# Gate and up projections as 2x2x2 Strassen block products, with weight sums kept in memory

## The chip, the cores and the metric

The kernel runs on one NeuronCore of a Trainium2 chip. The metric is the device time of the program in microseconds (us), as the median of several runs. The core has a matrix engine (TensorE, PE in the profile, with its weight loads as PEld), a vector engine (VectorE, DVE), a scalar engine (ScalarE, ACT), a general engine (GpSimd, POOL) and a sync engine (SyncE, SP), which here issues nearly all DMA transfers. Each engine runs its own instructions in a fixed order and waits on semaphores for the others.

## The reference

The input is x with 2048 rows (2 x 1024) of 1024 values; all data are fp32.

```python
s = silu(x @ w_gate.T)                      # 2048 x 2752
s[the 1376 smallest |s| of each row] = 0    # top-k by rows, k = 0.5 * 2752
s = s * (x @ w_up.T)
x = layernorm(x + s @ w_down.T)
# second part, with weights of a quarter of the width tiled four times,
# and low-rank terms of rank 2
g = silu(qlora(x, w1q, a1, b1)) * qlora(x, w3q, a3, b3)
x = layernorm(x + qlora(g, w2q, a2, b2))
```

The first part has the three large matrix products (2048 x 1024 x 2752 twice, and 2048 x 2752 x 1024); the second part needs a quarter of such work, because the tiled weights let the input be folded first.

## The kernel before, in words

Rows are worked in 16 tiles of 128, in four groups of four tiles (`GT`). The time line has three stages: gate and up for all groups, then the down projection with the first layer norm, then the second part (called FFN below).

**Precision.** TensorE multiplies in the reduced format fp32r. Each fp32 operand is therefore split in two: `split` (L162, L163) casts to fp32r on ScalarE (`xh`, `wh`) and subtracts the cast from the original for the residue (`xl`, `wl`), on GpSimd unless another engine is named. Each product is then three matmuls: high by high, low by high, high by low.

**Gate and up.** The 2752 columns are eight blocks of 344 (`BW`), the 1024 inputs are eight chunks of 128. For each group, each block and each of the two matrices, `gu_w` loads the weight block (three transfers of 3, 3 and 2 chunks), and splits it. `gate_up` then does 24 matmuls (L214) for each of the four tiles. Two tiles share a PSUM pair; there are three pairs. ScalarE takes gate's pair out of PSUM with Silu (L218), VectorE takes up's pair and multiplies it with the Silu result (L223), and both are stored in scratch memory (`s_d`, `m_d`). Weights are split anew for each group. A weight block is prepared while the one before it is multiplied.

**Top-k.** When a group's Silu results are stored, `topk` reads them back for four tiles. It looks for each row's threshold in six passes: three tiles are counted by ScalarE (L259), the fourth by VectorE (L256), and some ten instructions on 128x4 or 128x8 elements (L262 to L282) compute the next guess, for which the next pass waits. Then VectorE picks the exact threshold (L286, L287) and writes the mask (L298), stored as bf16. Top-k of a group runs beside gate and up of the next; the last group's runs beside the down projection.

**Down.** `down_load` (L447) multiplies a product tile by its mask on GpSimd, `down_prep` transposes it (L463) and splits it (L467, L468), and `down_mm` multiplies it with the split down weights (L483) and adds to an accumulator (L486). A small queue (`item`) runs loads two items and preparation some three items ahead.

**Order of the work.** The order in which each engine meets its instructions comes from the framework's scheduler, which works from the program order, the buffers of each pool and its own model of durations. It is fixed before the kernel runs.

Of the kernel before, what the change touches and what calls it, by code (L numbers as in the profile page):

```python
# [26 lines left out]
RW = 3 * BW  # L27
XS = 6
AHEAD = 5
DB = (512, 512, 512, 384, 384, 448)  # L30
GT = 4
EPS = 1e-5
# [4 lines left out]
TKAT = (5, 5, 5)  # L37
WARM = 14
TAILC = ((0, 512), (512, 768), (768, 1024))


class Kern:
# [6 lines left out]
    def run(self):  # L49
# [3 lines left out]
        with ExitStack() as es:  # L53
# [3 lines left out]
            self.sm = es.enter_context(tc.tile_pool(name="sm", bufs=4))  # L57
# [8 lines left out]
            self.k_d = [self.dram.tile([P, NI], BF, name=f"k_d{t}") for t in range(nt)]  # L66
            self.iota = self.const.tile([P, 8], F, name="iota")
            for i in range(8):
                nc.gpsimd.memset(self.iota[:, i : i + 1], 2.0 * i + 2.5)
            self.x_d = [self.dram.tile([P, H], F, name=f"x_d{t}") for t in range(nt)]  # L70
            tk_es, dp_es = ExitStack(), ExitStack()
            self.tk = tk_es.enter_context(tc.tile_pool(name="tk", bufs=1, side="right"))
            self.wp = es.enter_context(tc.tile_pool(name="wp", bufs=1))
            self.ev = es.enter_context(tc.tile_pool(name="ev", bufs=2))
            self.q1, self.q2, self.x2 = [], [], {}
            pst = es.enter_context(tc.tile_pool(name="pst", bufs=2, space=PSUM))
            self.tpb = lambda: pst.tile([P, 4, P], F, tag="tp", name="tp")
            gx_es = [ExitStack(), ExitStack()]
            psm = es.enter_context(tc.tile_pool(name="psm", bufs=3, space=PSUM))
            self.pair = lambda: psm.tile([P, 2, 512], F, tag="mm", name="mm")  # L80
            gx = [
                e.enter_context(tc.tile_pool(name=n, bufs=1, side=sd))
                for e, n, sd in zip(gx_es, ("gx1", "gx2"), ("right", "left"))
            ]
            self.xt = lambda sl, n: gx[sl // 4].tile([P, KC, P], R, tag=f"{n}{sl}", name=n)
            self.xr = gx[1]
# [3 lines left out]
            groups = self.groups(0)  # L90
            slots = self.x_slots(groups)
            d0 = self.down(0, early=3)
            hooks = {(g + 1, b): (lambda g=g: self.topk(g)) for g, b in enumerate(TKAT)}
            hooks[ng - 1, NB - 2] = lambda: next(d0)
            self.items = [(g, b, w) for g in range(ng) for b in range(NB) for w in "gu"]
            xs = self.x_load(groups[0], slots[0])
            for g in range(ng):
                if g == ng - 1:
                    gx_es[1].close()
                    self.dp = dp_es.enter_context(tc.tile_pool(name="dp", bufs=1, reuse_waits="tile"))  # L100
                nx = []
                for b in range(NB):
                    if b == NB - 2 and g + 1 < ng:
                        nx = self.x_load(groups[g + 1], slots[g + 1])
                    self.gate_up(g, b, groups[g], xs)
                    if (g, b) in hooks:
                        hooks[g, b]()
                xs = nx
            gx_es[0].close()
            self.dp2 = dp_es.enter_context(tc.tile_pool(name="dp2", bufs=1, reuse_waits="tile"))  # L110
            list(d0)
            for g in range(1, ng - 1):
                list(self.down(g, hooks={1: lambda: self.topk(ng - 1)} if g == 1 else {}))
            tk_es.close()
# [7 lines left out]

    def groups(self, g0):
        return [range(t, t + GT) for t in range(g0 * GT, self.nt, GT)]

    @staticmethod
    def x_slots(phases):
        free, last, res = list(range(XS)), [], []
        for g in phases:
            order = free + last  # L130
            use = order[: len(g)]
            free = [q for q in order if q not in use and q not in last]
# [32 lines left out]
    def x_load(self, tiles, slots):  # L165
        nc = self.nc
        xs = []
        for t, sl in zip(tiles, slots):
            if t == 2:
                self.nxt = self.gu_w(*self.items[0])  # L170
# [613 lines left out]
```

## Time and profile before

| What | Value |
|---|---|
| Runs before | 2018.61 to 2022.16 us, median 2019.07 (3 runs) |
| Profiled execution | 2021.57 us, of which the span from first to last instruction is 2019.8 |
| Gate and up, first to last matmul of L214 | 7.4 to 979 us |
| Down and first layer norm | to about 1555 us |
| TensorE busy | 1947.3 us, 96% of the span |
| VectorE, ScalarE, GpSimd busy | 1064.9, 897.5 and 1033.9 us |
| DMA | 389.64 MB, 193 GB/s on average |

All times in the profile are of one execution. Busy time of TensorE counts overlapping matmuls once; the length of one matmul in it is a latency, so the rate is to be read from counts in a stretch. A group line gives the source line, the engine, the operation, output and inputs, shape and count, then total busy time and the mean in ns of one, then the idle time just before these instructions and what ended it.

### The profile page before, as it was taken

How to read it: one execution, taken by the hardware profiler on the slowest of the kernel's cores; microseconds unless marked ns; L12 is line 12 of the kernel's file. 1: busy time of each engine (PE TensorE's matmuls, PEld its weight loads, DVE VectorE, ACT ScalarE, POOL GpSimd, SP SyncE). 2: the span in 40 equal slices, each digit the busy share in tenths (PEclk: the TensorE clock that was granted, in tenths of full speed). 3: DMA queues.
4: the chain of work that ended last, by engine and by line, in shares of the span. 5: the costliest groups of instructions: out<-in, count | busy, mean ns of one | idle time of the engine just before them, and what ended most of it. 6: DMA issues, size and time to landing. Idle time of an engine off the chain costs nothing. (4 is left out here: it accounts for less than half of the span.)

```text
span 2019.8 us, 29520 instructions
## 1 busy us (share of the span) xinstructions
PE 1947.3 (96%) x11117; PEld 1807.9 (90%) x11117; DVE 1064.9 (53%) x1581; ACT 897.5 (44%) x1472; POOL 1033.9 (51%) x694
## 2 busy tenths in 40 slices
PE   9999999999999999999988998999999899899998
PEld 9999999999999999999866786788877889899896
DVE  3000056602574024811479845644598987979565
ACT  4222396224952258322663113323323766747363
POOL 3343445454353444543556767555685744626162
PEclk9999999999999999999999998999999999999999
DMA  6555454575546555375644578655556748576561
GB/s 226 177 168 179 155 172 150 189 240 173 173 148 225 189 193 169 119 262 196 224 135 122 173 273 287 230 170 183 172 169 251 252 156 304 185 272 180 200 212 63
DMA packets 165886, 389.64 MB, mean 193 GB/s; under 512 B 16773, under 2 KB 76293, under 8 KB 165737
## 3 DMA queue, kind: packets, MB, share of 16 engines
q1 hardware_dynamic: 165592, 387.45, 57.9%
q8 instruction: 87, 1.43, 0.3%
q14 instruction: 63, 0.51, 0.1%
q10 hardware_dynamic: 144, 0.26, 0.0%
HBM read 297.94 MB, written 89.65 MB: 192 GB/s over the span
## 5 line engine op out<-in xcount | busy, mean ns | idle before, releaser
L163 POOL TENSOR_TENSOR wl<-wr,wh 128x1032 fp32r<-128x1032 f32 (+2 forms) x281 | 662.4, 2382 | 550.9 <-ACT wh L162 550.4
L214 PE MATMUL mm<-wh,xh 128*128 128x344 f32 x2048 | 650.1, 319 | 2.3 <-ACT xh L162 1.8
L214 PE MATMUL mm<-wl,xh 128*128 128x344 f32 x2048 | 651.3, 320 | 0.2 <-POOL wl L163 0.2
L214 PE MATMUL mm<-wh,xl 128*128 128x344 f32 x2048 | 650.7, 319 | 0.4 <-DVE xl L163 0.4
L162 ACT CAST wh<-wr 128x1032 fp32r<-128x1032 f32 (+2 forms) x289 | 274.5, 970 | 481.8 <-PE mm L214 270.3
L214 PEld LDWEIGHTS mm<-wh,xh 128*128 128x128 f32 x2048 | 385.1, 188 | 3.1 <-ACT xh L162 2.1
L214 PEld LDWEIGHTS mm<-wl,xh 128*128 128x128 f32 x2048 | 384.7, 188 | 0.5 <-POOL wl L163 0.4
L214 PEld LDWEIGHTS mm<-wh,xl 128*128 128x128 f32 x2048 | 384.0, 188 | 0.6 <-DVE xl L163 0.6
L223 DVE TENSOR_TENSOR sv<-mm,ev 128x688 f32<-128x688 f32 x64 | 55.5, 871 | 456.1 <-PE mm L214 360.6
L483 PE MATMUL mm<-wh,mh 128*128 128x512 f32 x704 | 231.7, 410 | 11.8 <-DVE acc L486 8.1
L483 PE MATMUL mm<-wl,mh 128*128 128x512 f32 x704 | 225.5, 401 | 10.2 <-POOL wl L163 10.2
L483 PE MATMUL mm<-wh,ml 128*128 128x512 f32 x672 | 213.5, 399 | 0.0
L259 ACT ACTIVATE k<-a,cur 128x2752 bf16<-128x2752 f32 x72 | 186.3, 2588 | 40.9 <-DVE cur L282 24.4
L447 POOL TENSOR_TENSOR m<-m,u 128x512 f32<-128x512 f32 (+2 forms) x96 | 110.6, 1158 | 149.8 <-DMA m<-m_d 94.7
L685 POOL TENSOR_TENSOR hf<-hf,gt 128x344 f32<-128x344 f32 x96 | 141.2, 1480 | 83.1 <-DVE gt L679 78.8
L672 PE MATMUL mm<-wh,fh 128*128 128x344 f32 x512 | 168.7, 330 | 14.3 <-DVE gt L679 8.8
L483 PEld LDWEIGHTS mm<-wl,mh 128*128 128x128 f32 x704 | 132.9, 191 | 43.3 <-POOL wl L163 13.0
L486 DVE TENSOR_TENSOR acc<-acc,mm 128x1024 f32<-128x1024 f32 x96 | 116.4, 1213 | 95.3 <-PE mm L483 94.5
L674 PE MATMUL mm<-wh,fl 128*128 128x344 f32 x512 | 165.7, 324 | 0.0
L673 PE MATMUL mm<-wl,fh 128*128 128x344 f32 x512 | 165.4, 323 | 0.0
L483 PEld LDWEIGHTS mm<-wh,mh 128*128 128x128 f32 x704 | 128.9, 192 | 38.6 <-issue 8.4
L483 PEld LDWEIGHTS mm<-wh,ml 128*128 128x128 f32 x672 | 128.0, 191 | 29.6
(153 smaller groups left out, 2494.4 us busy)
## 6 DMA issues: line engine op xcount, KB each, us to landing
wr<-wd SPq DMA_DIRECT2D x84, 512.0 KB
wr<-wg SPq DMA_DIRECT2D x64, 516.0 KB
wr<-wu SPq DMA_DIRECT2D x64, 516.0 KB
s_d<-ev SPq DMA_DIRECT2D x64, 344.0 KB
m_d<-sv SPq DMA_DIRECT2D x64, 344.0 KB
a<-s_d SPq DMA_DIRECT2D x64, 344.0 KB
wl<-wc_w SPq DMA_DIRECT2D x48, 344.0 KB
wh<-wc_w SPq DMA_DIRECT2D x48, 344.0 KB
```

The source lines that it names most:

```text
L162: self.nc.scalar.copy(hi, raw)
L163: (eng or self.nc.gpsimd).tensor_tensor(lo, raw, hi.bitcast(F), ALU.subtract)
L214: nc.tensor.matmul(o, l, r, start=n == 0, stop=n == len(ops) - 1)
L223: nc.vector.tensor_tensor(m, ps[:, :, :BW], sv[pr], ALU.mult)
L259: nc.scalar.activation(kv[2], av[j], AF.Sign, bias=t, scale=-1.0, accum_out=s)
L447: nc.gpsimd.tensor_tensor(m[:, :w], m[:, :w], u[:, :w], ALU.mult)
L483: nc.tensor.matmul(ps[:, h], a, b[:, h * 512 : (h + 1) * 512], start=i == 0, stop=i == len(ops) - 1)
L486: nc.vector.tensor_tensor(out, out, ps.rearrange("p a b -> p (a b)"), ALU.add)
L672: nc.tensor.matmul(o, fh[:, c, :], wh[:, c, :], start=c == 0, stop=False)
L673: nc.tensor.matmul(o, fh[:, c, :], wl[:, c, :], start=False, stop=False)
L674: nc.tensor.matmul(o, fl[:, c, :], wh[:, c, :], start=False, stop=False)
L685: G.tensor_tensor(hf[:, hs], hf[:, hs], gt, ALU.add)
```

## The change

The product of a 2 x 2 block matrix with another takes eight block products, or seven by Strassen's scheme (here in Winograd's form, with sums that build on each other). The change applies this to gate and up. The input's blocks are the two tiles of a pair (rows) by the two halves of the 1024 inputs; the weight's blocks are the two halves of the inputs by two neighbouring blocks of 344 columns. A *unit* is one matrix (`g` or `u`), two column blocks (`u`, four of them) and one group; it has seven *steps*, each one product for both tile pairs: 2 x 4 chunks x 3 = 24 matmuls into one PSUM pair.

- **Weights.** Each step has one operand of 128 x 1376 (four chunks of 344): three are quarters of the weight, four are sums T1 to T4 (`T_AT`), and all are split by `split` in `w_prep`, cast on ScalarE and residue on GpSimd, three steps ahead (`AHEAD`). In group 0 VectorE makes the sums from the four loaded quarters, and they are stored in scratch memory (`tw_d`); the other groups load them (`w_load`, six steps ahead, five raw buffers).
- **Input.** `x_slot` makes the sums S1 to S4 on VectorE for each pair and splits seven operands of 128 x 512, with the residue on VectorE.
- **Output.** `post` adds the products to four quarters of the result in SBUF: a copy on ScalarE at the first step and seven additions on VectorE after the others, each with one input from PSUM. `finish` applies Silu, or multiplies up's result with gate's, on 128 x 1376 in SBUF, and stores.
- **Buffers.** All of PSUM is used as four pairs in this stage. To make room, the top-k mask is kept as bytes instead of bf16; in the down stage ScalarE turns each mask tile into bf16 before GpSimd multiplies with it. Weight buffers come from rings (`Ring`); the sums and raw inputs borrow top-k's tiles. A few pools are smaller (`sm` three deep for four, the down stage's product tiles four for five).

The core of the diff; line by line it also replaces pools and tags.

```diff
-XS = 6
-AHEAD = 5
+NU = NB // 2
+KH = KC // 2
+CW = KH * BW
+AHEAD = 3
+LOADS = 6
...
+STEPS = (
+    ("A11", "B11"), ("S2", "T2"), ("S3", "T3"), ("S1", "T1"), ("A12", "B21"), ("S4", "B22"), ("A22", "T4"),
+)
+T_AT = ([("T1", "B12", "B11")], [("T2", "B22", "T1")], [("T3", "B22", "B12"), ("T4", "B21", "T2")], [], [], [], [])
...
+    def x_slot(self, g, op):
...
+            a11, a12, a21, a22, t = self.xraw[p]
+            if op == "S2":
+                V.tensor_tensor(t, a21, a22, ALU.add)
+                V.tensor_tensor(a21, a11, a21, ALU.subtract)
+                V.tensor_tensor(a11, t, a11, ALU.subtract)
+            elif op == "S4":
+                V.tensor_tensor(t, a12, a11, ALU.subtract)
+            src = {"A11": a11, "S2": a11, "S1": t, "A12": a12, "S3": a21, "S4": t, "A22": a22}[op]
+            hl = [self.xp.tile([P, KH, P], R, tag=f"{n}{op}{p}", name="x" + n) for n in "hl"]
+            self.split(*(x.rearrange("p a b -> p (a b)") for x in hl), src, V)
...
+    def w_load(self, i):
...
+        if g == 0:
+            if k == 0:
+                self.wb = {q: load(q) for q in ("B11", "B12", "B22", "B21")}
+            self.wraw.append(self.wb)
+        elif b[0] == "T":
+            r = self.wr.get()
+            nc.sync.dma_start(r, self.tw_d[w, u][:, int(b[1]) - 1])
+            self.wraw.append(r)
+        else:
+            self.wraw.append(load(b))
...
+    def w_prep(self, i):
...
+            for o, x, y in T_AT[k]:
+                V.tensor_tensor(tt[o], raw[x], raw.get(y, tt.get(y)), ALU.subtract)
+            if k == 2:
+                for j in range(2):
+                    nc.sync.dma_start(self.tw_d[w, u][:, 2 * j : 2 * j + 2], self.tt[j])
...
+        self.split(hi, lo, raw, V if b in LOV else nc.gpsimd)
...
+            for p in range(NPR):
+                xh, xl = self.xs[p, a]
+                ops[0] += [(p, x[:, q], wh[:, q]) for q in range(KH) for x in (xh, xl)]
+                ops[1] += [(p, xh[:, q], wl[:, q]) for q in range(KH)]
...
+        if k == 0:
+            nc.scalar.copy(c11, x)
+        elif k == 1:
+            V.tensor_tensor(c12, x, c11, ALU.add)
+        elif k == 2:
+            V.tensor_tensor(c21, x, c12, ALU.add)
+        elif k == 3:
+            V.tensor_tensor(c12, x, c12, ALU.add)
+            V.tensor_tensor(c22, x, c21, ALU.add)
+        elif k == 4:
+            V.tensor_tensor(c11, x, c11, ALU.add)
+        elif k == 5:
+            V.tensor_tensor(c12, x, c12, ALU.add)
+            self.finish(un, cc, 0)
+        else:
+            V.tensor_tensor(c21, x, c21, ALU.add)
+            self.finish(un, cc, 1)
...
+        if w == "g":
+            self.nc.scalar.activation(c, c, AF.Silu)
+        else:
+            s = cc[g, u, "g"][t].rearrange("p a b n -> p a (b n)")
+            self.nc.vector.tensor_tensor(c, c, s, ALU.mult)
...
         nc.sync.dma_start(m[:, :w], self.m_d[t][:, i0 : i0 + w])
         nc.sync.dma_start(u[:, :w], self.k_d[t][:, i0 : i0 + w])
-        nc.gpsimd.tensor_tensor(m[:, :w], m[:, :w], u[:, :w], ALU.mult)
+        nc.scalar.copy(ub[:, :w], u[:, :w])
+        nc.gpsimd.tensor_tensor(m[:, :w], m[:, :w], ub[:, :w], ALU.mult)
```

## The prediction

> **What bounds the kernel now.** I read the totals first, then busy time by stretch, the groups by shape for the engines that the change loads, the waits, and last single instructions of two engines side by side.
>
> ```profile
> PE 1947.3 (96%) x11117; PEld 1807.9 (90%) x11117; DVE 1064.9 (53%) x1581; ACT 897.5 (44%) x1472; POOL 1033.9 (51%) x694
> 100.00:200.00 100.00, 100.00 (x638) 100.00 (x637) 6.12 (x7) 23.05 (x28) 45.19 (x21) 1.00 0.54 173
> 300.00:400.00 100.00, 99.76 (x635) 99.47 (x634) 63.12 (x79) 44.35 (x44) 51.00 (x21) 1.00 0.48 156
> 1000.00:1100.00 100.00, 85.22 (x375) 66.53 (x374) 81.19 (x99) 53.72 (x55) 63.85 (x45) 0.95 0.46 139
> 1100.00:1200.00 100.00, 94.75 (x430) 76.17 (x429) 72.06 (x91) 21.79 (x31) 65.83 (x46) 0.97 0.62 211
> 1200.00:1300.00 100.00, 92.43 (x412) 73.80 (x411) 64.84 (x86) 30.58 (x42) 71.82 (x57) 0.95 0.80 268
> ```
>
> The first line is the totals. The others give, for a stretch, busy time and count of PE, PEld, DVE, ACT and POOL, then granted clock, DMA share and GB/s. Gate and up run from 7.4 to 979 us, and there TensorE is simply full: 638 matmuls in 100 us, one per 156.7 ns (the 319 ns of the groups is a pipelined latency). In the down stage from 1000 to 1300 us nobody is full, and PE still stands idle 9.2% of the time at a clock near 0.96.
>
> ```profile
> L163 POOL TENSOR_TENSOR wl<-wr,wh 128x1032 fp32r<-128x1032 f32 x124 | 307.1, 2496 | 493.9 <-ACT wh L162 493.8
> L163 POOL TENSOR_TENSOR wl<-wr,wh 128x688 fp32r<-128x688 f32 x72 | 142.6, 1980 | 23.2 <-ACT wh L162 23.2
> POOL wl L163 <- ACT wh L162: 550.4, 93, 16.3
> ```
>
> The residue of each weight is GpSimd's. Undisturbed, in the stretch 100 to 200, a block's three take 6.45 us (2.42 + 2.38 + 1.65). The last line, a wait, says that POOL has slack: it waits 550 us for the casts, which wait for TensorE.
>
> ```profile
> 332.72 1.38 DVE L262 TENSOR_SCALAR up<-cur 128x4 int32<-128x4 f32 x1 [6.70 <-ACT k L259]
> 334.02 1.72 DVE L263 TENSOR_SCALAR dn<-cur 128x4 int32<-128x4 f32 x1
> 339.17 0.87 DVE L223 TENSOR_TENSOR sv<-mm,ev 128x688 f32<-128x688 f32 x1
> 344.13 5.27 DVE L286 SCALAR_TENSOR_TENSOR k<-a,hi 128x2752 f32<-128x2752 f32 x1
> 353.15 3.08 DVE L286 SCALAR_TENSOR_TENSOR k<-a,hi 128x2752 f32<-128x2752 f32 x1
> ...
> 329.23 6.47 POOL L163 TENSOR_TENSOR wl<-wr,wh 128x1032 fp32r<-128x1032 f32 x3 [8.05 <-ACT wh L162]
> 341.72 9.23 POOL L163 TENSOR_TENSOR wl<-wr,wh 128x1032 fp32r<-128x1032 f32 x3 [6.02 <-ACT wh L162]
> ```
>
> These are start, duration and instruction in order of time. The same L286 takes 3.08 us alone and 5.27 beside POOL, while POOL's three grow from 6.47 to 9.23. Two instructions on four elements take 1.38 and 1.72: each ends when one of POOL's residues ends. So VectorE instructions of these kinds and POOL's two-input instructions take turns, whole instructions at a time. L223, with one input in PSUM, is 0.86 to 0.88 us in all 64 cases: it is not in the queue.
>
> **The Trainium skill.** "GPSIMD Engine Reference", section "Key points", says that GpSimd shares its SBUF interfaces with VectorE, with contention for VectorE instructions in a 2-port mode or with two SBUF inputs. The trace agrees (5.27 against 3.08). "VectorE: DVE Perf Modes", section "Mode 2×_2P", reserves the 2-port mode for one tensor in SBUF and excludes PSUM; the tiny L262 (delayed) and L223 (never) agree. "GPSIMD Engine Reference", section "Elementwise — side-by-side cycle accounting", puts the two-input floor at about 2.6 cycles an element; this trace's slope, (2.42 − 1.67) us over 344 elements, is 2.18 ns.
>
> **The change, step by step.** A unit is one matrix (gate or up), two column blocks and four tiles. It has seven products of 24 matmuls of the old shape.
>
> *TensorE.* 4 groups x 8 units x 168 = 5376 matmuls for 6144: 768 x 0.1567 = 120.3 us less, 842 for the stage; 3.76 us a product, 26.3 a unit.
>
> *GpSimd.* Before, two blocks need 2 x 6.45 = 12.9 us for 30.1 us of matmuls. Now each product has its own 128x1376 operand with its own residue, recomputed in every group: by the slope 2.43 + 0.75 = 3.18 us, 3.13 back to back, 21.9 a unit of 26.3. No such shape has run; the bounds are 2.98 (the skill's 2.6 cycles an element, at the 1.2 GHz of that page: an estimate) and 3.33 (1032-wide scaled by width). I take 3.13. For POOL alone that is hidden.
>
> *VectorE, not in the queue.* Seven PSUM additions a unit at 0.87 us (L223's shape; 0.80 back to back), 45 us a group, against 8 x 2 x 0.87 = 14 before.
>
> *VectorE, in the queue with POOL.* The final product of up is now SBUF by SBUF, 128x1376. The undisturbed 688 and 1032 rows on VectorE are 0.86 and 1.23, so about 1.59, say 1.5 in sequence: two per up unit, 1.5 a unit on average. In group 0 the four weight sums: 4 x 1.5 = 6.0 a unit. Input sums and residues: 22 of 128x512 a group at 0.62 = 13.6 us, by the order of the instructions half in the last unit of the group before and half in the first. Top-k is unchanged: 4 x 3.0 for L286 and some 65 tiny ones at 0.12, 20 us a group, in units 1 to 5 of groups 1 to 3, so 4.0 a unit.
>
> *Sum of the shared queue, where it exceeds TensorE's 26.3.* Group 0: the start costs 17 us (four weight quarters, 2.8 MB, stand on SP ahead of the input; with the first two input tiles 3.9 MB at the 266 GB/s of the first stretch is 14.6, then input sums, casts and residues), against 6.4 us lost before; unit 0 29; units 1 to 6 at 21.9 + 1.5 + 6.0 = 29.4; unit 7 with its share of inputs 36.2. Together 258. Groups 1 and 2: unit 0 30.2, five units at 21.9 + 1.5 + 4.0 = 27.4, unit 6 26.3, unit 7 30.2: 223.7 each. Group 3, with no inputs to follow, 219.8. Total 925.
>
> *Losses at hand-over.* That sum lets nobody ever wait in vain. But TensorE has 26.3 of 27.4 us to do, ScalarE in the top-k units about nine tenths (18 L259 at 2.7, 28 casts at 1.33, Silu and copies: 98 of 110 us), VectorE as much with its waits, and they run in fixed orders, three products ahead (four PSUM pairs, four weight buffers). A pass of top-k has about ten tiny instructions, each of which may stand behind one residue; behind them on VectorE stand the additions that free PSUM, and on ScalarE the next L259 waits for their result with the casts behind it. The nearest measured case of such coupling is the stretch 1000 to 1300: 9.2% lost, half clock included. Bounds 0 and 9.2%; I take 7%, 65 us. Gate and up would end at 990 instead of 979.
>
> *DMA.* A unit of groups 1 to 3 reads 4.9 MB of weights and sums and writes 1.4, with top-k's and the input's some 7.3 MB per 28 us, 260 GB/s; 268 at a share of 0.80 has been seen. I cost it at nothing; its cover is five raw buffers, about four products (15 us), and stores that wait for a late VectorE stand ahead of loads on SP. Without cover, each late load costs some 3 us.
>
> *Down stage.* The mask is now bytes and ScalarE widens it ahead of POOL's L447: 96 copies, by the 128x512 cast (584 ns) and its narrower forms 52 us on an engine 22 to 54% busy, but in front of the casts of L467 and in one buffer. POOL already waits 95 us there for m by DMA. Bounds 0 and 52; I take 8. FFN, buffers and the smaller pools: 0.
>
> Sum: 990 − 979 + 8 = +19 on a span of 2019.8. The profiled execution took 2021.6 (1.8 around the span), the median of the runs is 2019.1: I predict 2038.
>
> **The rivals.** (1) *TensorE stays the bound*: gate and up end at 17 + 842 + 3 = 862, time 2019.8 − 117 + 8 = 1911. For it: POOL alone is 83% loaded. Against: the turn-taking is in the trace, and group 0's 29.4 does not fit in 26.3. (2) *The queue binds but is well packed*, with 1 to 4% lost: 934 to 962, time 1983 to 2010. For it: buffers three deep, the order in group 0 gives each weight sum time before its residue is due. This is the other side; it decides below 4.9% loss (971 us). (3) *The tiny instructions bind*: a pass waits for all three residues that POOL is ahead, 9.4 us where I count about 4; 18 passes x 5.4 = 97 us, largely unhidden: time 2090 to 2130. For it: the pairs at 332.7 and 334.0. Against: with POOL no longer behind, its pauses let several through. (4) *The down stage loses more*: ScalarE waits for the mask with casts behind it, +30 to 50.
>
> **How the numbers follow.** Chances: forecast and its neighbours from 2000 up to 2070, 0.53; (2) 0.24; (1) 0.06; (3) 0.11; (4) on top of the forecast 0.06. The range 1972 to 2105 leaves out (1), a tail of (2) and the worst of (3), about 0.17. The likeliest case's own range is 2000 to 2070. A difference under 0.2% (4 us) can't be told from none here; that strip takes 0.07, mostly from the low end of the forecast. Of its 0.53, 0.08 lies below it. So faster is 0.24 + 0.06 + 0.08 = 0.38, same 0.07, slower the rest, 0.55.
>
> **What would show it.** POOL's 128x1376 residue: undisturbed 3.1 to 3.25 us, mean above 3.6. VectorE's four-element instructions in gate and up often at 1 to 3 us. The matmul rate in units 1 to 6 of group 0 is about 570 in 100 us (168 in 29.4 us), not 638, and PE waits for wl there. A matmul interval other than 156.7 ns, a residue under 2.9 us, or VectorE's sums undelayed beside POOL would make this wrong; a rate of 638 through group 0 means rival (1), PE waiting mostly for VectorE's additions after 300 us means (3).

## The result and the profile after

The changed kernel takes 2145.06 us (median; 2144.39 to 2145.88) beside 2020.62 us of the kernel before: a ratio of 1.0614, with a 95% interval of 1.0596 to 1.0633. The forecast was 2038 us in a range of 1972 to 2105. The direction was right, the size was not: the loss is 124 us, not 19.

The stages by their matmuls, from the profiled executions (spans 2019.8 and 2143.9 us):

| us | before | after | difference |
|---|---|---|---|
| start of gate and up, until the first matmul | 7.4 | 18.8 | |
| end of gate and up | 979.3 | 1078.7 | +99.4 |
| down and first layer norm | 567.4 | 584.5 | +17.1 |
| second part, first group | 130.6 | 139.1 | +8.5 |
| second part, the other groups | 333.0 | 332.7 | −0.3 |

Within gate and up the four groups took 244.9, 242.0, 242.0 and 243.0 us before, and 257.0, 277.7, 264.2 and 261.0 after.

From the page of the changed kernel, the totals and the granted clock by fortieths of the span:

```profile
PE 1887.8 (88%) x10349; PEld 1736.1 (81%) x10349; DVE 1566.9 (73%) x1891; ACT 1091.4 (51%) x1646; POOL 1391.7 (65%) x730
...
PEclk8999999989999899998999999999999989999999
```

VectorE has gained 502 us of busy time (1064.9 before) and GpSimd 358 (1033.9 before); TensorE has lost 60, and its clock is no longer full in gate and up. Two stretches of gate and up, in group 0 and in group 1 (columns as in the prediction: PE, PEld, DVE, ACT, POOL, clock, DMA share, GB/s):

```profile
100.00:200.00 100.00, 86.40 (x513) 85.58 (x512) 74.89 (x39) 35.25 (x29) 87.53 (x23) 0.93 0.64 242
400.00:500.00 100.00, 76.31 (x454) 74.95 (x453) 88.63 (x67) 37.88 (x31) 70.47 (x21) 0.90 0.54 181
```

Before, each of these had about 638 matmuls. VectorE is now the busiest engine in the second of them, and much of that is not work but waiting inside instructions, as the groups by shape show (busy time, mean ns, then idle time before):

```profile
L165 POOL TENSOR_TENSOR wl<-wr,wh 128x1376 fp32r<-128x1376 f32 x192 | 667.8, 3498 | 248.3 <-ACT wh L164 225.6 <-PE mm L265 17.0 <-DMA a<-s_d 4.7
...
L354 DVE TENSOR_SCALAR up<-cur 128x4 int32<-128x4 f32 x48 | 47.7, 1002 | 40.4 <-ACT jk L351 40.3
```

The last line is top-k's comparison on four elements: 1002 ns on average, with a smallest value of 154. Before, it was L262, with 467 on average:

```profile
L262 DVE TENSOR_SCALAR up<-cur 128x4 int32<-128x4 f32 x48 | 22.0, 467 | 112.4 <-ACT k L259 112.4
```

Summed over all VectorE instructions of gate and up, the time above the shortest instance of the same instruction is 84, 82, 79 and 65 us in the four groups (the first counted from the start of the span).

What this does to TensorE is seen best where its largest pause of group 1 lies. Timeline of the changed kernel, VectorE, then TensorE, then GpSimd, with start and duration (a GpSimd or PE line of several merges instructions that follow at once):

```profile
415.47 3.65 DVE L312 TENSOR_TENSOR cc<-cc,cc 128x1376 f32<-128x1376 f32 x1
419.04 3.13 DVE L354 TENSOR_SCALAR up<-cur 128x4 int32<-128x4 f32 x1
422.08 0.16 DVE L355 TENSOR_SCALAR dn<-cur 128x4 int32<-128x4 f32 x1
422.15 3.09 DVE L354 TENSOR_SCALAR up<-cur 128x4 int32<-128x4 f32 x1
425.15 0.16 DVE L355 TENSOR_SCALAR dn<-cur 128x4 int32<-128x4 f32 x1
425.28 3.00 DVE L356 COPY_PREDICATED hi<-up,cur 128x8 f32<-128x8 int32 x1
428.20 0.16 DVE L357 COPY_PREDICATED lo<-dn,cur 128x8 f32<-128x8 int32 x1
428.32 5.86 DVE L378 SCALAR_TENSOR_TENSOR ku<-a,hi 128x2752 f32<-128x2752 f32 x1
434.10 0.18 DVE L382 TENSOR_TENSOR df<-iota,hi 128x32 f32<-128x32 f32 x1
434.23 0.86 DVE L290 TENSOR_TENSOR cc<-mm,cc 128x688 f32<-128x688 f32 x1
...
421.95 1.42 PE L265 MATMUL mm<-wl,xh 128*128 128x344 f32 x8
435.14 0.65 PE L265 MATMUL mm<-wh,xh 128*128 128x344 f32 x1 [11.77 <-DVE cc L290]
...
413.86 17.45 POOL L165 TENSOR_TENSOR wl<-wr,wh 128x1376 fp32r<-128x1376 f32 x5 [0.65 <-ACT wh L164]
```

GpSimd runs five residues without a pause. Three instructions of VectorE on four or eight elements wait for one whole residue each (3.13, 3.09, 3.00 us), and L378 for one too (5.86 instead of 3.0). Only then comes L290, the addition that takes a finished product out of PSUM. It needs nothing from GpSimd and takes 0.86 us, but it stands behind the others in VectorE's fixed order, and TensorE stands still for 11.8 us. The same pause comes in groups 2 and 3 at the same product (12.6 and 11.8 us).

A second pause comes in the next unit of each of these groups (9.2, 9.5 and 9.2 us), and its reason is another one. There VectorE writes the mask with four instructions L390 in a row:

```profile
467.59 3.07 DVE L390 TENSOR_SCALAR_CACHE_REDUCE ku<-a,thr 128x2752 uint8<-128x2752 f32 x1
...
480.37 0.86 DVE L295 TENSOR_TENSOR cc<-mm,cc 128x688 f32<-128x688 f32 x1
```

Each of the four takes 3.07 to 3.08 us, as in all other places, so none of them waits for GpSimd. They are 12 us long together, and the addition L295, for which TensorE waits, stands behind them. The kernel before has the same row (L298, from 368.06 to 380.15) with PSUM's L223 behind it, and TensorE waited for L223 no more than 0.5 us in the whole stage:

```profile
380.07 1.65 DVE L223 TENSOR_TENSOR sv<-mm,ev 128x688 f32<-128x688 f32 x2
```

L290 belongs to the second product of the unit (`k == 1`), and TensorE waits for it ahead of the fifth. With four PSUM pairs the fifth would need only the first product's pair, which ScalarE had emptied at 418.2 (L288). So three pairs are in use. That holds for the whole stage: of 221 products only the very last starts before the addition (or copy) three products earlier has ended, 58 start within 0.3 us after it, and none starts less than 3.9 us after the one four products earlier. The code has a reason at hand: the warm-up's matmuls take one half of a pair through `tp_half`, and the other half stays in `self.half` until the down stage's first transposes at the end of group 3.

A pair also lasts for less time than before. It was filled by 48 matmuls, 7.5 us, and is filled by 24 now, 3.76 us. With three pairs an addition may come as late as two more products take: by this estimate 15 us before and 7.5 us now. The row of L390 fits into the first and not into the second.

The waits of the changed kernel (total, times, longest) name the same place; the last three belong to the down stage, read later:

```profile
PE mm L265 <- DVE cc L290: 61.4, 12, 12.6
PE mm L265 <- DVE cc L295: 36.7, 6, 9.5
...
ACT ub L543 <- POOL m L544: 178.9, 65, 8.1
POOL m L544 <- DMA m<-m_d: 81.6, 29, 8.1
POOL m L544 <- ACT ub L543: 38.0, 20, 7.4
```

Gate and up's 1060 us from first to last matmul are 5376 matmuls at 156.7 ns, 842 us; 166 us in 51 pauses of more than 0.5 us; 41 us in some 300 intervals at half clock (about 0.29 us instead of 0.157); and 11 us of small lengthenings. 155 us of the pauses, in 46 places, end within 0.3 us of the addition three products earlier. The half clock follows the pauses. The Trainium skill, "TensorE: Matmul & The Clock Gate", section "What's actually happening", says that the clock is halved after an idle window of some 3.4 us. The trace agrees in the size of the steps: the half-clock stretches here last 3.4, 6.8, 10.2 or 13.7 us, and one of 20.5 at the start; before there was none in this stage. It doesn't agree in the idle time that it takes: pauses of 2.4, 2.8, 2.8 and 2.8 us were followed by half clock too, though one of 2.9 and one of 3.2 were not.

So three questions are open: is it the turns at the shared interface that TensorE pays for, or something else of the change (DMA, ScalarE); which of the users of the interface cost most; and where do the 17 and 8.5 us of the later stages come from.

### The profile page after: what moved, and what is told of

It is laid out like the page before. It is cut to its first block, busy times and chain, and to the rows that moved or that the text cites. A ratio compares the mean times of both kernels' runs of the same rounds, so it can differ in the third digit from the quotient of the medians.

```text
span 2143.9 us, 28910 instructions
## 1 busy us (share of the span) xinstructions
PE 1887.8 (88%) x10349; PEld 1736.1 (81%) x10349; DVE 1566.9 (73%) x1891; ACT 1091.4 (51%) x1646; POOL 1391.7 (65%) x730
## 5 line engine op out<-in xcount | busy, mean ns | idle before, releaser
L165 POOL TENSOR_TENSOR wl<-wr,wh 128x1376 fp32r<-128x1376 f32 (+2 forms) x285 | 897.5, 3167 | 308.6 <-ACT wh L164 285.5
L265 PE MATMUL mm<-wh,xh 128*128 128x344 f32 x1792 | 595.4, 336 | 159.6 <-DVE cc L290 61.4
L265 PE MATMUL mm<-wh,xl 128*128 128x344 f32 x1792 | 589.9, 333 | 6.3 <-DVE xl L165 6.3
L164 ACT CAST wh<-wr 128x1376 fp32r<-128x1376 f32 (+2 forms) x289 | 350.6, 1225 | 301.4 <-PE mm L265 166.1
L265 PEld LDWEIGHTS mm<-wh,xh 128*128 128x128 f32 x1792 | 356.9, 199 | 172.9 <-DVE cc L290 62.8
L265 PE MATMUL mm<-wl,xh 128*128 128x344 f32 x1792 | 323.0, 323 | 3.0 <-POOL wl L165 3.0
L265 PEld LDWEIGHTS mm<-wl,xh 128*128 128x128 f32 x1792 | 294.3, 190 | 3.3 <-POOL wl L165 3.3
L351 ACT ACTIVATE jk<-a,cur 128x2752 int8<-128x2752 f32 x72 | 186.3, 2588 | 104.2 <-DVE cur L374 46.9
L544 POOL TENSOR_TENSOR m<-m,ub 128x512 f32<-128x512 f32 (+2 forms) x93 | 112.5, 1210 | 141.1 <-DMA m<-m_d 81.6
L543 ACT CAST ub<-u 128x512 bf16<-128x512 uint8 (+2 forms) x93 | 53.1, 571 | 194.5 <-POOL m L544 178.9
```

The costliest lines, as they stand in the source:

```text
L164: self.nc.scalar.copy(hi, raw)
L165: (eng or self.nc.gpsimd).tensor_tensor(lo, raw, hi.bitcast(F), ALU.subtract)
L265: nc.tensor.matmul(ps[:, p], l, r, start=n[p] == 0, stop=n[p] == 3 * KH - 1)
L351: nc.scalar.activation(jk.bitcast(I8), av[j], AF.Sign, bias=t, scale=-1.0, accum_out=s)
L543: nc.scalar.copy(ub[:, :w], u[:, :w])
L544: nc.gpsimd.tensor_tensor(m[:, :w], m[:, :w], ub[:, :w], ALU.mult)
```

## The experiments

The theory, called P in some of the expectations: VectorE and GpSimd take turns by whole instructions, and TensorE is late because of these turns. Its rivals are that TensorE waits for casts or loads whatever the interface does, and that it is the new work as such, on VectorE or ScalarE, that is too much. Times of gate and up are those of the profiled execution; a number for a group is from its first matmul to that of the next. The units of a group are counted from 0. The kernel before, run beside each, took 2021.9 to 2026.4 us (medians). Except for b1 and f1 each experiment is one run; single runs of the kernel before lie between 2017 and 2034 us, so a difference of less than some 10 us between two single runs says little.

### Is it the turns? (a1, a2, a3)

The residue on GpSimd cut to a quarter of its width, all else as it was:

```diff
-        self.split(hi, lo, raw, V if b in LOV else nc.gpsimd)
+        nc.scalar.copy(hi, raw)
+        nc.gpsimd.tensor_tensor(lo[:, :BW], raw[:, :BW], hi[:, :BW].bitcast(F), ALU.subtract)
...
-    ops[1] += [(p, xh[:, q], wl[:, q]) for q in range(KH)]
+    ops[1] += [(p, xh[:, q], wl[:, 0]) for q in range(KH)]
```

> The changed kernel, but GpSimd forms the residue of only the first 344 of each 1376 weight columns, and the high-by-low matmuls use that piece for all four chunks (same matmuls, same casts and loads; values differ). This leaves out three quarters of the residue, and GpSimd's turn at the shared queue falls from 3.1 to about 0.9 us a product. Theory P (VectorE is late because its two-input and tiny instructions stand behind residues): the additions come in time, gate and up end at 870 to 900 us instead of 1079, time 1935 to 1970. Rival O (VectorE is late because long top-k instructions stand ahead of the additions in its fixed order, port or not): the idle times of TensorE in front of the fifth product of unit 4 and the seventh of unit 5 stay at 6 to 10 us, groups 1 to 3 stay above 235 us each, time 2030 or more.

1935.16 us. Gate and up end at 890.2; the groups take 219.1, 218.7, 212.8 and 225.2. VectorE and ScalarE have the same instructions as in the changed kernel, and DMA the same loads. Groups by shape of this kernel:

```profile
L236 POOL TENSOR_TENSOR wl<-wr,wh 128x344 fp32r<-128x344 f32 x192 | 214.6, 1118 | 529.4 <-ACT wh L235 495.1 <-PE mm L266 17.6 <-DMA a<-s_d 10.3
...
L355 DVE TENSOR_SCALAR up<-cur 128x4 int32<-128x4 f32 x48 | 14.9, 320 | 19.4 <-ACT jk L352 19.3
```

Top-k's comparison falls from 1002 to 320 ns, though nothing of it was changed, and the stage shrinks by 189 us, to within 34 us of TensorE's own 842. The saving of TensorE is real. What gives it back is GpSimd's residue, and neither ScalarE's load nor DMA; whether as a turn or as GpSimd's own work is left to the next run.

Top-k left out for groups 0 to 2 (`topk` writes a constant mask and returns):

```diff
+        if g < 3:
+            ...   # constant mask to k_d
+            return
```

> The changed kernel without top-k for groups 0 to 2 (their mask is zero; top-k of group 3, in the down stage, stays). Residues, sums and additions are untouched. Theory T (the loss in groups 1 to 3 is top-k's instructions on VectorE, with the PSUM additions behind them): groups 1 to 3 take 215 to 230 us each instead of 278, 264 and 261, group 0 stays at 257, time 2000 to 2030. Rival S (residues and the change's own VectorE work are enough): groups 1 to 3 stay above 245 us, time above 2085.

1980.65 us; gate and up end at 941.7. Group 0 is 261.6; groups 1 to 3 are 221.2, 221.4 and 218.7, which is 57, 43 and 42 us less than with top-k, 142 in all (group 0, in which nothing was left out, is 4.6 longer). The whole time lies below the 2000 to 2030 expected, because the down stage is 24 us shorter as well. In the windows of this kernel:

```profile
300.00:400.00 100.00, 99.31 (x629) 99.06 (x628) 46.99 (x38) 46.04 (x39) 94.33 (x31) 1.00 0.86 306
```

GpSimd is 94% busy and TensorE is full: a unit in the middle of a group takes 26.4 to 26.6 us, as the forecast's 26.3 for TensorE alone. The residues by themselves bind nothing here, and neither do three PSUM pairs: by the same test this kernel uses no more, and its pauses are 7 to 8 us in each of groups 1 to 3. DMA moves 306 GB/s at a share of 0.86, about as much as in the busiest such stretch of the changed kernel (310 at 0.84, from 500 to 600 us), and TensorE doesn't wait: the forecast's nothing for DMA stands.

The four weight sums of group 0 made by ScalarE as copies, so that VectorE has none (with other values top-k of groups 0 to 3 takes its exact search, some 650 us each, and only group 0 is to be read):

```diff
-    V.tensor_tensor(tt[o], raw[x], raw.get(y, tt.get(y)), ALU.subtract)
+    nc.scalar.copy(tt[o], raw[x])
```

> The changed kernel, with the four weight sums of group 0 replaced by plain copies of one quarter on ScalarE (values differ; same buffers, stores and loads). It takes 32 instructions of 128x1376 off VectorE and the shared queue. By the sum of the shared queue (29.4 us a unit with the sums, 23.4 without, 26.3 for TensorE), group 0 falls from 257 to 225 to 235 us and the rest does not move: time 2112 to 2125. Rival (group 0 is held by its start and half clock): less than 10 us.

Group 0 takes 221.4 us instead of 257.0 (whole time 4725.62). The sums cost 36 us, somewhat more than the 22 to 32 that the sum over the shared queue had given; without them units 1 to 7 of the group take 26.6 us each.

### Which part of top-k? (c1, c2, s1)

The ten small instructions of a pass replaced by one (L378 and the counts stay; the guesses are no longer a search):

```diff
-            up, dn = ...            # compare, two predicated copies, secant step
-            ...
+            nxt = pair("cur")
+            V.scalar_tensor_tensor(nxt[:, 0], cur[:, 1], 0.0, cur[:, 0], ALU.mult, ALU.add)
+            cur = nxt
```

> The changed kernel with top-k's chain of small instructions after each pass (L354 to L374, about eleven on 128x4 or 128x8 elements) replaced by one instruction that copies the old guess; it leaves out the search, so the mask is another one, and the exact fallback is left out too. Counts on ScalarE and VectorE, the picks (L378, L379), the mask (L390) stay. Top-k costs groups 1 to 3 57, 43 and 42 us (against the run without it). If the small instructions waiting for residues are the larger part, groups 1 to 3 fall by 25 to 45 us each, time 2020 to 2070. If the long instructions are (ten of 3 us in units 4 and 5), they fall by less than 15 each, time above 2100.

2033.14 us; groups 257.9, 242.6, 238.7 and 234.9. Groups 1 to 3 give back 35, 26 and 26 us: 87 of top-k's 142. What is left has its largest pauses, 6.4, 7.2 and 7.1 us, in unit 5 behind the four instructions that write the mask (in group 1 with one turn behind them).

L378, two inputs on 128x2752, replaced by a form with one input that accumulates:

```diff
-    V.scalar_tensor_tensor(b, av[j], hi[:, 0, j : j + 1], av[j], ALU.is_lt, ALU.mult)
+    V.tensor_scalar(b, av[j], hi[:, 0, j : j + 1], None, ALU.is_lt, ALU.add, accum_out=d[:, j : j + 1])
```

> The changed kernel with the four two-input instructions L378 of each top-k replaced by one-input comparisons with a count, the form of L390, which is 3.08 us whatever GpSimd does (values differ; the exact fallback is left out). It takes 4 x 3.0 us a group off the shared queue and 5.6 us of waits a group off VectorE, and keeps the length of what stands ahead of the additions. Port theory: groups 1 to 3 fall by 6 to 15 us each, time 2100 to 2125. If only the length counts: less than 5 each, time above 2130.

2123.32 us; groups 1 to 3 gain 4, 2 and 6 us, less than expected in two of the three. The new form has the same length and no turn, so this is what the turns of the four large instructions cost. It is much less than what a group's sixty small ones cost (c1), although each of the four takes 3.0 us undisturbed and a small one about 0.15.

The same search with about half the small instructions (32 for 59 in the interface's queue):

```diff
-    for q in range(2):
-        V.tensor_scalar(up[:, q], cur[:, 1], 0.0, None, ALU.is_gt)
-        V.tensor_scalar(dn[:, q], cur[:, 1], 0.0, None, ALU.is_le)
-    V.copy_predicated(hi, up, cur)
-    V.copy_predicated(lo, dn, cur)
+    V.scalar_tensor_tensor(up..., cur[:, 1, None, :].to_broadcast([P, 4, GT]), 0.0, self.side, ALU.is_gt, ALU.not_equal)
+    V.copy_predicated(hl, up, cur[:, None].to_broadcast([P, 2, 2, GT]))
...  # and one instruction less in the secant step
```

> The changed kernel, same computation, with top-k's chain written in fewer instructions: one comparison and one predicated copy update both brackets (two for six), and the guess of the later passes takes four two-input instructions for five; about 32 small port instructions a group for 59. The run with the chain reduced to one instruction gained 86 us in groups 1 to 3. If the gain goes by the number of small instructions, half of them are gone: groups 1 to 3 10 to 20 us shorter each, time 2095 to 2125. If two or three waits a pass remain whatever the number, less than 5 each, time above 2130.

2120.79 us; groups 1 to 3 gain 4, 1 and 7 us, far below the half of 87 (the other half of the 24 us falls outside them). The count of small instructions is therefore not the measure. In the timeline above only three of six waited for a residue; every second one slipped through (0.16). Which of them the shorter chain spares was not traced one by one.

### How long is a turn? (c3, c4, d1, d2, d3)

The residue in two halves of 688, with the same work on GpSimd plus one more start each:

```diff
-        self.split(hi, lo, raw, V if b in LOV else nc.gpsimd)
+        nc.scalar.copy(hi, raw)
+        for c in (slice(0, CW // 2), slice(CW // 2, CW)):
+            nc.gpsimd.tensor_tensor(lo[:, c], raw[:, c], hi[:, c].bitcast(F), ALU.subtract)
```

> The changed kernel, same computation, with each residue formed by two instructions of 128x688 instead of one of 128x1376. GpSimd's turn falls from 3.1 to 1.65 us, its total rises from 21.9 to about 23.1 us a unit. If VectorE's waits for whole turns are what costs (65 to 82 us of waits a group in groups 1 to 3), they fall by a third to a half and groups 1 to 3 take 235 to 255 us each, group 0 255 to 270, time 2070 to 2115. If only the sum of the shared queue counts, it is longer by 1.2 us a unit, and the time is 2145 to 2185.

2095.38 us, 50 less; groups 249.0, 264.3, 252.8 and 249.5. The same place of the timeline in this kernel:

```profile
406.36 1.33 DVE L356 TENSOR_SCALAR up<-cur 128x4 int32<-128x4 f32 x1 [0.24 <-ACT jk L353]
...
407.68 1.66 DVE L356 TENSOR_SCALAR up<-cur 128x4 int32<-128x4 f32 x1
...
409.37 1.60 DVE L358 COPY_PREDICATED hi<-up,cur 128x8 f32<-128x8 int32 x1
```

1.33, 1.66 and 1.60 where 3.13, 3.09 and 3.00 stood. The work is the same and only the length of GpSimd's turn is halved: this shows the mechanism most directly. The pauses behind the mask's row, which has no turns, stay at 6.7 to 7.4 us.

Two of the seven residues moved to VectorE, where one took 1.8 us on average and GpSimd's takes 3.1 undisturbed:

```diff
-LOV = ()
+LOV = ("B22", "T4")
```

> The changed kernel, same computation, with two of the seven residues of each unit (quarters B22 and T4) formed by VectorE. The shared queue falls by 2 x (3.13 - 1.5) = 3.3 us a unit, VectorE gets 3 us a unit more, before waits. If the sum of the shared queue is the limit, gate and up end 50 to 100 us earlier, time 2045 to 2095. If VectorE is the limit, with its waits, the time is 2140 to 2200.

2090.01 us, 55 less; groups 243.4, 246.6, 259.7 and 265.0.

Both together, then with the shorter chain, then with three residues (`"B21"` too) on VectorE:

> The changed kernel, same computation, with residues in halves on GpSimd and two of seven residues on VectorE together. Alone they gave 50 and 55 us. If they act on different things (length of a turn, sum of the queue), 80 to 105 together: time 2040 to 2065. If both only relieve the same waits, 60 to 75: 2070 to 2085.

2046.92 us, 98 less: the two gains add up almost fully. Gate and up end at 987.0.

> As the run before, with the shorter chain as well. By the sum of the three 2010 to 2045; 2040 to 2065 if the waits of the chain are already short with half turns.

2047.48 us: with short turns the shorter chain is worth nothing that one run could show.

> As the run before, with three of seven residues on VectorE. Shared queue 24.8 us a unit in group 0 and some 20 without sums, VectorE about 19 us a unit before top-k and waits. If the queue still limits group 0, it falls to 225 to 238 us and the time is 5 to 20 us under the run before; if VectorE's own work now limits units 1 to 5, groups 1 to 3 are longer and the time is the same or up to 30 longer.

2023.31 us; groups 229.8, 233.5, 239.7 and 254.0. From unit 1 on, group 0 now runs at TensorE's own pace, 26.4 to 26.7 us a unit, sums included. Gate and up end at 974.2, five us earlier than before the change.

### Input on GpSimd, and an earlier start (e1, e2, e3)

From d3, the input residues of groups 1 to 3 on GpSimd instead of VectorE:

```diff
-    self.split(..., src, V)
+    self.split(..., src, nc.gpsimd if g else V)
```

> The run with half turns, the short chain and three of seven residues on VectorE (2023 us), with the input residues of groups 1 to 3 formed by GpSimd instead of VectorE; same computation. If VectorE's own load and waits now limit groups 1 to 3 (it is 75 to 96% busy there, GpSimd about 55%), each falls by 4 to 12 us: time 1995 to 2012. If the shared queue limits, it is longer by about 8 us a group: 2030 to 2050.

2034.29 us, 11 more; groups 228.1, 242.3, 249.1 and 252.6. Taking work from VectorE, the busier engine, brought nothing. A residue of 128x512 takes 1.26 us from GpSimd undisturbed and 1.72 on average, where VectorE needs 0.68 and 1.01, which speaks for the shared queue. The place doesn't: in group 1, units 7 and 0, in which residues moved, are 1.2 and 1.5 us shorter, and the lengthening lies in units 3, 5 and 6, in which none did. That the queue limits here is not shown.

From e1, the input loaded ahead of the second half of the first weight quarters; then fewer residues on VectorE after group 0. In both, groups 1 to 3 work on stale input, with which top-k takes its exact search; only group 0 is to be read.

```diff
+    for j, q in enumerate(("B11", "B12", "B22", "B21")):
+        if i == 0 and j < 2:
+            self.x_raw(0, j)        # the two input tiles of a pair
+        self.wb[q] = load(q)
```

> As the run before, with the first input tiles loaded ahead of the later weight quarters, and the weight sums thus behind the first input splits on VectorE; same computation. In the run it builds on, the first 50 us hold 129 matmuls (20 us of work) at a clock of 0.74. If the order of loads is what delays the start, group 0 ends 5 to 12 us earlier, the rest does not move. If the shared queue fills up in unit 0 anyway, less than 3.

> As the run before, with two of seven residues on VectorE in groups 1 to 3 and three in group 0; same computation. If VectorE's load limits groups 1 to 3, they are 3 to 10 us shorter each; if the sum of the shared queue does, 3 to 10 longer (the step from two to three gave 23 us in all, 19 of it in groups 1 to 3).

The first matmul of e2 comes at 8.8 instead of 17.4 us, and group 0 ends at 246.2 us, as without it (245.5). The 8.6 us are gone again soon: the first 50 us of the span hold 124 matmuls, and 132 without the edit. An earlier first matmul alone brings nothing here. e3's group 0 ends at 245.3; what it was made for, the later groups, can't be read from it.

### The later stages: mask and smaller pools (b1, b3)

The kernel before with the byte mask and ScalarE's widening as its only change:

```diff
-    u = self.dp.tile([P, 512], BF, tag="u", bufs=2, name="u")
+    u = self.dp.tile([P, 512], U8, tag="u", bufs=2, name="u")
+    ub = self.dp.tile([P, 512], BF, tag="ub", bufs=1, name="ub")
...
+    nc.scalar.copy(ub[:, :w], u[:, :w])
-    nc.gpsimd.tensor_tensor(m[:, :w], m[:, :w], u[:, :w], ALU.mult)
+    nc.gpsimd.tensor_tensor(m[:, :w], m[:, :w], ub[:, :w], ALU.mult)
```

> The kernel before, with only the mask kept as bytes and widened by ScalarE ahead of GpSimd's product in the down stage. If this is what lost 17 us in the down stage, the time is 2030 to 2042; if the stage lost them by other means (fewer product buffers, a late start), 2018 to 2026. The forecast had 8 us for it.

2018.14 us beside 2024.63: a ratio of 0.9967, interval 0.9958 to 0.9976. The down stage takes 561.4 us instead of 567.4. This is faster than both kernels. The waits of this kernel:

```profile
ACT ub L449 <- POOL m L450: 171.4, 63, 13.8
POOL m L450 <- DMA m<-m_d: 82.8, 28, 6.4
...
POOL m L450 <- ACT ub L449: 40.3, 22, 7.1
```

GpSimd waits 40 us for the widened mask, but it waits less for the product (82.8; 94.7 before) and no longer for the mask's own transfer (20.6 before). ScalarE stands 171 us waiting for the one buffer `ub`, and that costs nothing. In the changed kernel these waits are nearly the same (38.0, 81.6 and 178.9), so the mask is not where its 17 us went either.

b1 with the smaller pools of the change (`sm` three deep, product tiles four, weights of the second part in the weight pool):

```diff
-    self.sm = es.enter_context(tc.tile_pool(name="sm", bufs=4))
+    self.sm = es.enter_context(tc.tile_pool(name="sm", bufs=3))
...
-    tag="m", bufs=2 if x else 3
+    tag="m", bufs=1 if x else 3
```

> The kernel before with the byte mask and the smaller pools of the change: small tiles three deep for four, product tiles of the down stage four for five, raw weights of the second part from the down weights' three buffers. If these cost the 8 us in the first group of the second part (139 against 131) and the 17 in the down stage (584 against 567), they show here: 2030 to 2042. If not, 2014 to 2022, and what was lost after gate and up comes from how that stage ends.

2022.02 us. The down stage takes 563.7, so the pools are nothing there. The second part's first group takes 136.1 where b1 has 130.9: about five of the 8.5 us.

### A second split of the input (g1, f1)

The changed kernel holds a piece that the forecast had overlooked. In the last unit of a group `x_slot` splits all seven operands of the next group, and the first step of that group loads and splits A11 once more. That makes 28 input transfers of 512 KB where 16 would do, and 62 residues `xl` where there would be 56. Without it:

```diff
-            if (u, w, k) == (0, "g", 0) and g + 1 <= ng and g:
-                self.x_slot(g, a)
```

> The changed kernel, but without the second load and split of A11 at the first step of groups 1 to 3 (two transfers of 512 KB per pair, and per group two casts on ScalarE and two residues of 128x512 on VectorE less; the split of the last unit of the group before is used). Nothing of the computation is left out. If the shared interface and VectorE's order set the pace, about two residues at 1 to 2 us with their waits go per group: 2 to 4 us a group, time 2133 to 2140. If the late DMA of these loads (2 MB ahead of weight loads on SP) is what holds the first unit of each group, 6 to 10 us a group: 2115 to 2127. If it is hidden: 2145.

2124.2 us, 21 less; 13.3 of it in gate and up (groups 258.4, 264.5, 256.5 and 267.2) and 7 in the down stage. The total fits the theory of loads that hold the first unit, but its place doesn't: the first unit of the groups takes 33.6, 31.5 and 41.3 us, no shorter than with it (33.5, 26.5, 29.6). Shorter are units 4 and 5, in which nothing was removed. The timeline there:

```profile
402.84 0.66 DVE L352 TENSOR_SCALAR up<-cur 128x4 int32<-128x4 f32 x1 [1.13 <-ACT jk L349]
...
403.48 0.16 DVE L352 TENSOR_SCALAR up<-cur 128x4 int32<-128x4 f32 x1
...
403.67 0.17 DVE L354 COPY_PREDICATED hi<-up,cur 128x8 f32<-128x8 int32 x1
403.87 3.08 DVE L376 SCALAR_TENSOR_TENSOR ku<-a,hi 128x2752 f32<-128x2752 f32 x1
```

The chain ahead of the first large instruction took 9.3 us in the changed kernel and 1.0 here: it met a pause of 0.65 us between two runs of residues on GpSimd. Most of this gain is a matter of which instructions meet, and it can't be called the price of the second split.

The same edit in d3:

> The version of the changed kernel with three of seven residues on VectorE, the other four in halves on GpSimd and the shorter chain of top-k (2023 us), without the second load and split of A11 in groups 1 to 3. Nothing of the computation is left out. There TensorE waits less, so by the pace of the shared interface 1 to 3 us a group: 2014 to 2020, about the kernel before. If the loads hold the first unit: 2000 to 2010, faster than before. If hidden: 2023.

2017.3 us beside 2021.85: a ratio of 0.9977, interval 0.9965 to 0.9989. Gate and up end at 967.9. Two stretches, of group 0 and of group 1:

```profile
60.00:240.00 180.00, 179.91 (x1147) 179.59 (x1146) 141.99 (x108) 83.97 (x72) 116.88 (x52) 1.00 0.75 277
300.00:480.00 180.00, 161.47 (x990) 159.94 (x990) 150.12 (x141) 98.73 (x83) 94.31 (x48) 0.96 0.69 241
```

In group 0 TensorE is full. In the groups with top-k it still loses time: 990 matmuls in group 1's stretch are a seventh fewer, and the longest pauses behind the mask's row are 3.9 to 5.5 us. With the change's whole scheme kept, this version is faster than the kernel before by about 0.2%, and b1, without the scheme, by 0.3%.

## Why the prediction was wrong

**TensorE: right.** 5376 matmuls at 156.7 ns, 842 us. a1 comes to 876 us for the stage from its first matmul on, and units without disturbance take 26.4 to 26.6 (26.3 forecast).

**GpSimd's residue: right.** 3.08 to 3.17 us undisturbed against 3.13 to 3.18; the mean of 3.50 is a little under the "above 3.6" given as a sign.

**The sum of the shared queue: right in total in group 0, there partly by luck, and right without top-k.** Group 0 ends at 275.8, and the forecast's 258 with its 7% is 276. The parts differ and cancel: unit 0 took 40.3 for 29, units 1 to 6 on average 31.7 for 29.4, unit 7 took 26.6 for 36.2. The matmul rate in 100 to 200 us was 513, not 570, and the sums cost 36 us in a3, where this sum gives 22 to 32. The same sum with top-k's turns left out gives 218 us for groups 1 and 2 (30.2 + 6 x 26.3 + 30.2) and 214 for group 3; a2 has 221, 221 and 219.

**Losses at hand-over: this is the step that failed.** In groups 1 to 3 the forecast gave top-k 1.1 us in each of five units, and 7% for everything that waits in vain, about 21 us a group together. Groups 1 to 3 took 38, 25 and 26 us more than the forecast with its 7%, which is the whole miss in gate and up; a2 puts top-k's part at 57, 43 and 42. The sum took a small instruction at 0.12 us and supposed that its waiting hides (the sum "lets nobody ever wait in vain"), with 7% for the rest from a stage that has other instructions. The runs show that a pass stands behind several whole residues (from 419.0 to 434.2 in the timeline above, 15 us), that PSUM's additions stand behind it in VectorE's order, and that TensorE then stops for up to 12.6 us and goes on at half clock. The cover was smaller than taken, too: "three products ahead" with "four PSUM pairs" are two products with three pairs in the trace, 7.5 us. A row of long instructions of top-k that takes no turn, 12 us of mask, is no longer hidden by that; the forecast had nothing for it. How much of the 155 us the fourth would save was not tried; a pair is 3.76 us of matmuls, so by this estimate it can take at most that from each of the 46 pauses, 104 us in all. Where small instructions wait for whole residues, this is rival (3). It was given 0.11, because "with POOL no longer behind, its pauses let several through". That reason fails in the timeline: POOL had no pause for 17.45 us. Rival (3)'s 97 us for 18 passes stands beside the 87 that c1 gives back; its range, 2090 to 2130, still ends below the 2145. The other 55 of top-k's 142 are settled only in part: in c1 about 20 are pauses behind the mask's row, L378 has some 12 (c2), and the rest, in which ScalarE's counts and the casts behind them may share, was not taken apart.

**DMA at nothing: right.** a2 moved 306 GB/s without a wait of TensorE. The count of inputs was wrong by six splits and twelve transfers (g1).

**The down stage: wrong in its reason.** The mask was put at +8 and is −6 (b1). The stage lost 17 us all the same. Neither mask nor pools make them (b1, b3). Variants with an easier end of gate and up have less (a2 560, c1 558, a1 565, f1 567), but g1, c4 and d1 (577, 576, 578) ended earlier too, d1 at 987 us, and have more than half of it. Its cause stays open.

**FFN and pools at nothing: wrong by 8.5 us**, of which the smaller pools have about five.

As a sum: +99 instead of +11 in gate and up, +17 instead of +8 in the down stage, +8.5 instead of 0.

## What to carry to other kernels

Before giving GpSimd longer instructions, list what VectorE does beside it in forms that share its interface, and allow each small one up to one whole GpSimd instruction, not its own length (in the rows shown here about every second one paid it); then see what stands behind it in VectorE's order and who waits for that. If the work must stay on GpSimd, cut it into short instructions: halving their length gave back 50 us here for one more start each. A busy total doesn't show this, because the waiting counts as busy time: compare the mean of an instruction with its minimum.

When a change makes the products smaller, work out anew how late an addition may come: half as many matmuls in a PSUM pair are half the cover, and a row of VectorE instructions that was hidden before may no longer be.

## What the runs showed of the hardware

- Long GpSimd instructions delay small VectorE ones by up to their own full length: 3.13 us for an instruction that takes 0.15 alone, and 1.3 to 1.7 us with GpSimd's halved. In the rows shown, several that follow each other alternate: one waits for a residue, the next slips through (0.16), the next waits again.
- The Trainium skill, "SBUF — State Buffer", section "SBUF: two separate sides", calls the shared pair of ports an exclusive lock that is held for the whole instruction; the traces agree (5.86 us for an L378 that takes 3.0).
- `COPY_PREDICATED` with eight elements waited like the others (3.00 us). A one-input form with an accumulator (L390, 3.07 to 3.08 us in all 16 cases), MAX8 (3.01 to 3.03) and everything with an input in PSUM (0.85 to 0.88) did not.
- TensorE's longer pauses cost more than themselves: in gate and up 41 us at half clock beside 166 us of pauses. Half clock came with every pause of 3.3 us or more and after four of 2.4 to 2.8; after one of 2.9 and one of 3.2 it did not come.
- The same kernel with 12 loads and six splits less ran 21 us faster, mostly in places where nothing had been removed. With turns of 3 us, a change of a few microseconds in when instructions meet moves a group by 5 to 15 us; differences between single groups of that size are not to be explained one by one.
